# The second layer of a two-layer network woven between the first layer's mixtures, on one core

## The chip, the core and the metric

The kernel runs on one core of one Trainium2 chip. Its engines work side by side: PE (TensorE, matrix products into PSUM), DVE (VectorE), ACT (ScalarE), POOL (GpSimd) and SP, which issues most of the DMAs. Each engine takes its own instructions in order, and waits for the others through semaphores. The metric is the device time of one execution in microseconds.

## What is computed

4096 tokens of 128 numbers pass two layers. Each layer normalizes x, makes an attention-like signal s and a gate from a mixture of eight experts (the two best of eight for each token), and adds s * silu(gate) to x. In layer one s is linear attention; in layer two it is a recurrence that learns a matrix by one gradient step per token.

```python
xn = _layernorm(x)
s = _L0_attn_ref(xn, ...)          # relu(q)+eps, relu(k)+eps; q (k'v) z, times W_out, + b_out
g = _silu(_L0_ffn_ref(xn, ...))    # 8 experts of width 64, the 2 best
x = x + s * g
xn = _layernorm(x)
s = _L1_attn_ref(xn, ...)          # per token: pred = W k + b; g = 2/128 (pred - v)
                                   # W -= 0.01 g k'; b -= 0.01 g; out = W q + b   (from W0, b0)
g = _silu(_L1_ffn_ref(xn, ...))    # 8 experts of width 512, the 2 best
x = x + s * g
```

## The kernel before

The tokens lie in eight groups of 512 (`G`), each four tiles of 128; a group holds two sequences of 256.

**First layer.** `norm0` (L299) takes the statistics of a group on DVE (`stats`, L261), the root on ACT, normalizes on ACT into xn and turns it on PE into xnT (`turned`, L276). `attention` (L492) makes q (L494 on PE, evicted as qT by DVE at L496), then k and v tile by tile (kvp, L503; k by DVE, v by ACT), k'v (kw, L514) and s (sp, L520; s by DVE, L525). Its product also holds the logits of the first gate. After four groups `gate0` (L390) picks the two best experts on DVE and leaves `mask` and the factor `u`. `mixture0` (L531) turns the mask on PE (mp, L534), copies it twice on ACT (off, mT), computes all experts' hidden layers (hp: L543, with a small product, L547, that pushes unpicked experts down, then Gelu on ACT, L548), then the result (yp, L552 and L553). ACT scales it and takes its Tanh, and three DVE operations (L560 to L562) update x.

**Second layer, first part.** `second` (L792) works on a pair of groups: `norm1` (L317) takes the statistics on DVE, finds the root by Newton steps there (`inverse_root`, L284), normalizes on ACT into xw, turns it, and multiplies with WRO (rp, L343): the residual R and the output O of the recurrence's start, and the logits. A second product (L345, 24 rows, bfloat16) adds b0, split in three bfloat16 parts by `prepare` (L197). ACT copies rp to RO (L346). `dispatch` (L409) picks the two best experts on DVE, counts tokens per expert by products with triangles of ones (cp, L426 to L430), and computes each token's place. POOL then writes the rows of xw to these places with 16 indirect DMAs (L456). `keys` (L570) makes K (projk), Q (projq) and K'K (kk, L582), stored through `kk_hbm`. After each second pair `invert_blocks` (L592) inverts 32x32 blocks of four groups on DVE in 31 dependent steps.

**Second layer, second part.** `solve` (L619) runs the recurrence of a group in 14 steps of small products with DVE between them. `fetch`, `turn`, `hidden` and `result` take the slots of 256 dispatched tokens through one expert each, 39 in all; the steps of `solve` for groups 2 to 7 lie between them. Groups 0 and 1 are solved ahead of the slots. At the end the rows are gathered and x is updated (L851 to L853).

**Order.** The framework's planner orders each engine's instructions by its own estimate of when they are ready, starting from the order in which they are emitted. The emission (L776 to L807) is: attention of all eight groups with the gates after groups 3 and 7, then mixture 0, 1, 2, then for g = 2, 4, 6 the second layer's pair (g - 2, g - 1) after mixture g, and the last pair at the end. SP's queue holds, in order, the loads, the copies of the second layer's weights to `wts` (L154 to L160), 43 writes of zeros to `rows` (L166), then the traffic of `kk_hbm`, the blocks and the slots. Tiles come from pools with few buffers each: PSUM has three banks for h (kvp, hp, rp), two for y and three for t (turned tiles, mp, projk, projq, kk, cp), so a product also waits for an earlier eviction.

Of the kernel before, what the change touches and what calls it, by code (L numbers as in the profile page):

```python
# [21 lines left out]
P = 128  # L22
E = 8
# [32 lines left out]
def _constants():  # L56

    s = np.arange(P)[:, None]
    t = np.arange(P)[None, :]
    out = [t // BLK < s // BLK, s <= t]
    sel = np.zeros((P, 4 * P), bool)
    for e in range(E):  # L70
        sel[e, e * 64:(e + 1) * 64] = True
    out.append(sel)
    for row in (E - np.arange(E), np.arange(E * BATCH) % BATCH > 0, np.arange(NS), np.arange(E) * CAP * SLOT):
        out.append(np.broadcast_to(row[None, :], (P, row.size)))
    out.append(np.concatenate([s // E == np.arange(3), s % E == 0], axis=1))
    return np.concatenate(out, axis=1).astype(np.float32)
# [3 lines left out]
def tile_kernel(  # L80
# [57 lines left out]
    bias3 = p2.tile([3 * E, 2 * P], F32, tag="xgT", name="bias3")  # L138
    for k in range(3):
        nc.sync.dma_start(out=bias3[ts(k, E), 0:P], in_=b2_0)  # L140
# [4 lines left out]
    nc.sync.dma_start(out=bias3[:, P:], in_=b0.partition_broadcast(3 * E))  # L145
# [36 lines left out]
    third = consts_sb[0:3 * E, ds(at + 2 * E + E * BATCH + NS, 4)]  # L182
# [10 lines left out]
    starts = wp.tile([3 * E, P], BF16, tag="starts", name="starts")  # L193

    B0 = wp.tile([3 * E, 2 * P + E], BF16, tag="B0", name="B0")

    def prepare():  # L197

        n = 3 * E

        hi, mid = (p2.tile([n, 2 * P], BF16, tag=t, name=f"third_{t}") for t in ("e0", "e1"))
        a, acc = (p2.tile([n, 2 * P], F32, tag=t, name=f"third_{t}") for t in ("R2", "y"))
        V = nc.gpsimd
        V.tensor_copy(hi, bias3)
        V.tensor_tensor(a, bias3, hi, ALU.subtract)
        V.tensor_copy(mid, a)
        V.tensor_tensor(a, a, mid, ALU.subtract)
        V.tensor_scalar(acc, hi, third[:, 0:1], None, ALU.mult)
        V.tensor_scalar(bias3, mid, third[:, 1:2], None, ALU.mult)
        V.tensor_tensor(acc, acc, bias3, ALU.add)  # L210
        V.tensor_scalar(a, a, third[:, 2:3], None, ALU.mult)
        V.tensor_tensor(B2, acc[:, 0:P], a[:, 0:P], ALU.add)
        V.memset(B0, 0.0)
        for k in range(2):
            V.tensor_tensor(B0[:, ts(k, P)], acc[:, P:], a[:, P:], ALU.add)
        V.tensor_copy(starts, third[:, 3:4].to_broadcast([n, P]))
        V, late = nc.vector, tc.keep_in_program_order
        late(V.tensor_tensor(strict, upto, ident, ALU.subtract))

        late(V.tensor_scalar(sel_off, sel_sb, OFF, None, ALU.mult))  # L220

        for j in (1, 3):
            late(V.tensor_scalar(mKQ[:, j, :], upto, -ETA, None, ALU.mult))
        late(V.tensor_copy(free, region))
# [45 lines left out]
    def centre(mv, rstd, n):  # L270

        nb = p3.tile([P, n], F32, tag=f"nb{n}", name="nb")
        nc.vector.scalar_tensor_tensor(nb, mv[:, :, 0], -1.0, rstd, ALU.mult, ALU.mult)
        return nb
# [24 lines left out]
    def norm0(g):  # L299
        mv = p3.tile([P, 4, 2], F32, tag="mv", name=f"mv0_{g}")  # L300
        stats(g, mv, pinned=g > 0)
        if g == 0:

            rstd = inverse_root(mv[:, :, 1], 4)
        else:
            rstd = p3.tile([P, 4], F32, tag="rstd", name=f"rstd0_{g}")
            nc.scalar.activation(rstd, mv[:, :, 1], AF.Sqrt, bias=eps_t)
            nc.vector.reciprocal(rstd, rstd)
        nb = centre(mv, rstd, 4)
        xn = p2.tile([P, 4, P], F32, tag="xn", name=f"xn0_{g}")  # L310
        for i in range(4):
            nc.scalar.activation(
                xn[:, i, :], X[g][:, i, :], AF.Identity, bias=nb[:, i:i + 1], scale=rstd[:, i:i + 1]
            )
        return turned(0, g, xn)

    def norm1(q):  # L317

        mv = p3.tile([P, BATCH, 2], F32, tag="mv1", name=f"mv1_{q}")
        for h in range(2):  # L320
            stats(2 * q + h, mv[:, ts(h, 4), :])
        rstd = inverse_root(mv[:, :, 1], BATCH)
        nb = centre(mv, rstd, BATCH)
        out = []
        for h in range(2):
            g = 2 * q + h

            XW[g] = p3.tile([P, 2, 4, ROW], F32, tag="xw", name=f"xw{g}", bufs=4)
            xn = XW[g][:, 0, :, 0:P]
            for i in range(4):  # L330
                j = 4 * h + i
                nc.scalar.activation(  # L332
                    xn[:, i, :], X[g][:, i, :], AF.Identity, bias=nb[:, j:j + 1], scale=rstd[:, j:j + 1]
                )
            xnT = turned(1, g, xn)
            nc.gpsimd.tensor_copy(XW[g][:, 1, :, 0:P], xn)
            for k in range(2):
                nc.gpsimd.tensor_copy(XW[g][:, k, :, ROW - 1].bitcast(I32), to[:, ts(g, 4), k])
            if h == 0:
                RO = keep.tile([P, BATCH, 2 * P + E], F32, tag=f"RO{q}", name=f"RO{q}")  # L340
            for i in range(4):
                rp = ps_h.tile([P, 2 * P + E], F32, tag="h", name=f"rp{g}_{i}")
                nc.tensor.matmul(rp, lhsT=xnT[:, i, :], rhs=WRO, start=True, stop=False)  # L343

                nc.tensor.matmul(rp, lhsT=starts, rhs=B0, start=False, stop=True)  # L345
                nc.scalar.copy(RO[:, 4 * h + i, :], rp)  # L346
            out.append((xnT, RO[:, ts(h, 4), :]))
        return out, RO[:, :, 2 * P:].rearrange("p i e -> p e i")

# [59 lines left out]
    def dispatch(q, L):  # L409
# [14 lines left out]
        V.tensor_tensor(V1, SC, S, ALU.subtract)  # L424
        cp = ps_t.tile([P, E * n + E], F32, tag="t", name=f"cp{q}")
        nc.tensor.matmul(cp[:, 0:E * n], lhsT=strict, rhs=S.rearrange("p e i -> p (e i)"), start=True, stop=False)  # L426
        nc.tensor.matmul(cp[:, 0:E * n], lhsT=ones_sq, rhs=V1.rearrange("p e i -> p (e i)"), start=False, stop=True)
        last = tl("d_last", [P, E])
        V.tensor_copy(last, SC[:, :, n - 1])
# [62 lines left out]
    def attention(g, xnT, logits):  # L492
# [3 lines left out]
        nc.vector.tensor_scalar(qT, qp, 0.0, ATT_EPS, ALU.max, ALU.add)  # L496
# [31 lines left out]
        return s  # L528


    def mixture0(g, xnT, s, mask, u):  # L531
# [8 lines left out]
        hT2 = [p2.tile([P, 2, 4, P], F32, tag="hT", name=f"hT0_{g}_{h}") for h in range(2)]  # L540
        for q in range(4):
            hp = ps_h.tile([P, 4, P], F32, tag="h", name=f"hp0_{g}_{q}")
            nc.tensor.matmul(  # L543
                hp, lhsT=w1_0sb[:, ts(q, 2), :].rearrange("p e h -> p (e h)"), rhs=xnT, start=True, stop=False
            )

            nc.tensor.matmul(hp, lhsT=sel_off[:, ts(q, P)], rhs=off, start=False, stop=True)  # L547
            nc.scalar.activation(hT2[q // 2][:, q % 2], hp, AF.Gelu, bias=b1_0sb[:, q:q + 1])  # L548
        yp = ps_y.tile([P, 4, P], F32, tag="y", name=f"yp0_{g}")
# [5 lines left out]
        f = p2.tile([P, 4, P], F32, tag="U", name=f"f0_{g}")  # L555
        t = p2.tile([P, 4, P], F32, tag="T", name=f"t0_{g}")
# [13 lines left out]
    def keys(g, xnT):  # L570
# [5 lines left out]
        nc.scalar.copy(K, pp)  # L576
        qp = ps_t.tile([P, 4, P], F32, tag="t", name="projq" + n)
# [8 lines left out]
        return K  # L586
# [32 lines left out]
    def solve(g, Q, K, RO):  # L619
# [3 lines left out]
        D = DT[g % 3]  # L623
        for i in range(NB):
            q = ts(i, BLK)
            nc.sync.dma_start(out=D[q, :, q], in_=blk_by[g // 4, i, :, ts(g % 4, 4), :])
# [141 lines left out]
    def some(work, n):  # L768
        for _ in range(n):
            next(work, None)  # L770
# [4 lines left out]
    xnT0, s0, S0 = [], [], {}  # L775
    for g in range(G):  # L776
        if g % 4 == 0:
            logits0 = p2.tile([P, E, NT // 2], F32, tag="logits0", name=f"logits0_{g}")
        while len(xnT0) < min(g + 3, G):
            xnT0.append(norm0(len(xnT0)))  # L780
        s0.append(attention(g, xnT0[g], logits0))
        if g == 1:
            prepare()
        if g % 4 == 3:
            gate0(g // 4, logits0, mask, u)
    for j, th in enumerate((thK_sb, thQ_sb)):
        merged(j, th)


    XW, first, K1, blocks = {}, [], [], []  # L790

    def second(q):  # L792
        pair, logits = norm1(q)
        first.extend(pair)
        dispatch(q, logits)
        K1.extend(keys(g, first[g][0]) for g in (2 * q, 2 * q + 1))
        if q % 2:
            blocks.append(invert_blocks(q // 2))

    for g in range(G):  # L800
        mixture0(g, xnT0[g], s0[g], mask, u)
        if g >= 2 and g % 2 == 0:
            second(g // 2 - 1)
        if blocks:
            some(blocks[0], 10)
    some(blocks[0], BLK)
    second(G // 2 - 1)  # L807


# [85 lines left out]
```

## Time and profile before

| what | value |
|---|---|
| median of three runs | 533.08 us (531.45 to 534.18) |
| the profiled execution | 532.66 us, span 530.9 us |
| busy: PE, PEld, DVE, ACT, POOL | 444.9, 335.9, 261.7, 205.6, 161.5 us |
| attention, to about 77 us | PE busy 55.3 us |
| mixtures with the second layer's first part, 77 to 281 us | PE busy 177.2 us |
| slots, 307 to 500 us | PE busy 190.6 us |
| end, 500 to 531 us | PE busy 4.4 us |

PEld is the loading of weights into PE, which overlaps with products. A float32 product shows as two matmul records. In a timeline a row has start, length, engine, line and operation, output and inputs, count, and in brackets the idle time before it with the engine that ended it. In a group a row has the busy time, the mean in ns, and the idle time before. The clock of PE is given as a share of full speed, 1.00 or 0.50 at any moment, and in between as a mean.

### The profile page before, as it was taken

The numbers are of one execution on the slowest core, as the hardware profiler recorded it, in microseconds if no ns is written. First come the engines' busy times: TensorE is split into PE (matmuls) and PEld (weight loads), VectorE is DVE, ScalarE is ACT, GpSimd is POOL, SyncE is SP. The second block draws the span as 40 slices with busy tenths as digits, with TensorE's granted clock in tenths as the row PEclk, the third lists the DMA queues.
The fourth block names the chain that finished last, engine by engine and source line by source line (L and its number), as shares of the span: only waits on it lengthen the run. The fifth ranks groups of instructions, "written<-read, shape, count | busy, mean of one in ns | idle before, by whom it ended". The sixth has DMA issues, their size and how long they took to land.

```text
span 530.9 us, 7732 instructions
## 1 busy us (share of the span) xinstructions
PE 444.9 (84%) x2471; PEld 335.9 (63%) x2471; DVE 261.7 (49%) x1000; ACT 205.6 (39%) x476; POOL 161.5 (30%) x215
## 2 busy tenths in 40 slices
PE   2956999989989997993879499999999999999900
PEld 1635765634543563351358489999999989989900
DVE  4567573424160437574065149964445334334447
ACT  4455455442552535154221034333334423333321
POOL 3410000010750372037127214433424233434500
PEclk9997999967995997696569699999999999999965
DMA  9689997000310120022002575685766555545185
GB/s 237 154 166 299 393 392 280 1 0 2 125 35 1 60 71 11 0 72 77 7 30 81 178 191 155 194 238 149 225 191 187 144 171 155 186 145 178 36 313 166
DMA packets 59404, 75.64 MB, mean 142 GB/s; under 512 B 17100, under 2 KB 42364, under 8 KB 59364
## 3 DMA queue, kind: packets, MB, share of 16 engines
q1 hardware_dynamic: 51268, 62.30, 38.7%
q0 software_dynamic: 4544, 9.38, 5.1%
q10 hardware_dynamic: 3552, 3.48, 1.9%
q8 instruction: 19, 0.31, 0.2%
q14 instruction: 21, 0.17, 0.1%
HBM read 43.81 MB, written 36.06 MB: 150 GB/s over the span
## 4 chain that ended last, share of the span: by engine, by line
PE 57%; DMA 19%; SPq 8%; DVE 7%; ACT 4%; issue 3%; POOL 1%; ACTq 0%; DVEq 0%; POOLq 0%
PE yp L735 9%; PE hp L723 9%; DMA xg<-rows 9%; PE rp L343 7%; PE yp L552 7%; PE hp L543 6%; SPq L166 5%; DMA wts<-in_w_dram 4%; PE rp L345 2%; DMA fk<-res 2%; PE projq L578 2%; PE kk L582 2%; PE projk L574 2%; PE tp L279 1%; PE hp L547 1%
## 5 line engine op out<-in xcount | busy, mean ns | idle before, releaser
L744 POOL DMA_INDIRECT res<-y,go x78 | 75.7, 971 | 133.4 <-DVE y L742 109.3
L726 ACT ACTIVATE hT<-hp,wt 128x256 f32<-128x256 f32 x156 | 64.5, 470 | 113.7 <-issue 73.3
L456 POOL DMA_INDIRECT rows<-xw,place x64 | 63.0, 985 | 104.3 <-DVE xw L449 86.0
L735 PE MATMUL yp<-wt,hT 128*128 128x128 f32 x624 | 76.0, 275 | 0.0
L723 PE MATMUL hp<-xgT,wt 128*128 128x256 f32 x312 | 74.1, 381 | 1.9 <-DVE xgT L714 1.6
L735 PEld LDWEIGHTS yp<-wt,hT 128*128 128x128 f32 x624 | 72.8, 192 | 0.1
L723 PEld LDWEIGHTS hp<-xgT,wt 128*128 128x128 f32 x312 | 56.4, 190 | 8.9 <-DVE xgT L714 2.6
L343 PE MATMUL rp<-WRO,xnT 128*128 128x264 f32 x64 | 38.8, 709 | 4.0 <-ACT xnT L281 4.0
L543 PE MATMUL hp<-xnT,w_0sb 128*128 128x512 f32 x64 | 39.5, 728 | 1.4 <-ACT hT L548 1.4
L552 PE MATMUL yp<-w_0sb,hT 128*128 128x128 f32 x256 | 38.4, 290 | 0.0
L708 DVE COPY go<-xg 128x2 f32<-128x2 f32 x39 | 6.8, 175 | 63.6 <-DMA xg<-rows 63.5
L552 PEld LDWEIGHTS yp<-w_0sb,hT 128*128 128x128 f32 x256 | 31.7, 191 | 5.0 <-issue 2.8
L560 DVE SCALAR_TENSOR_TENSOR f<-t,f 128x512 f32<-128x512 f32 x8 | 5.5, 693 | 45.3 <-ACT t L559 45.3
L346 ACT COPY RO<-rp 128x264 f32<-128x264 f32 x32 | 12.1, 378 | 34.7 <-PE rp L345 34.7
L363 DVE TENSOR_REDUCE d_m_d<-RO 128x8 f32<-128x64 f32 x4 | 0.9, 220 | 46.8 <-ACT RO L346 46.8
L548 ACT ACTIVATE hT<-hp,b_0sb 128x512 f32<-128x512 f32 x32 | 21.1, 688 | 5.2 <-PE hp L547 4.9
L343 PEld LDWEIGHTS rp<-WRO,xnT 128*128 128x128 f32 x64 | 15.4, 299 | 11.9 <-ACT xnT L281 6.4
L740 DVE TENSOR_TENSOR y<-yp,wt 128x256 f32<-128x256 f32 x39 | 16.3, 419 | 12.1 <-PE yp L735 12.1
L279 PE MATMUL tp<-ident,xw 128*128 128x128 f32 x32 | 10.2, 394 | 14.4 <-ACT xw L332 14.1
L503 PE MATMUL kvp<-WKVG,xnT 128*128 128x264 f32 x64 | 19.6, 423 | 2.8 <-ACT v L505 2.3
L608 DVE TENSOR_TENSOR inv<-NBK,TB 64x31 f32<-64x31 f32 (+15 forms) x62 | 21.1, 341 | 0.8
L714 DVE COPY xgT<-xp 128x256 f32<-128x256 f32 x39 | 16.2, 416 | 10.6 <-PE xp L712 9.0
(239 smaller groups left out, 779.7 us busy)
## 6 DMA issues: line engine op xcount, KB each, us to landing
wt<-wts SPq DMA_DIRECT2D x39, 578.0 KB
rows<-pad SPq DMA_DIRECT2D x43, 390.0 KB
xg<-rows SPq DMA_DIRECT2D x39, 130.0 KB
wts<-in_w_dram SPq DMA_DIRECT2D x16, 256.0 KB
x<-in_x_dram SPq DMA_DIRECT2D x8, 256.0 KB
kk_hbm<-cb SPq DMA_DIRECT2D x8, 256.0 KB
B<-kk_hbm SPq DMA_DIRECT2D x8, 256.0 KB
fk<-res ACTq DMA_DIRECT2D x4, 512.0 KB
```

The lines of the kernel that those rows point to most:

```text
L166: nc.sync.dma_start(out=rows_q[q], in_=pad)
L343: nc.tensor.matmul(rp, lhsT=xnT[:, i, :], rhs=WRO, start=True, stop=False)
L456: nc.gpsimd.indirect_dma_start(out=parts_r[2 * (BATCH * q + i) + k], out_offset=IndirectOffsetOnAxis(ap=place[:, k, i:i + 1], axis=0), in_ ...
L503: nc.tensor.matmul(kvp, lhsT=xnT[:, i, :], rhs=WKVG, start=True, stop=True)
L543: nc.tensor.matmul(hp, lhsT=w1_0sb[:, ts(q, 2), :].rearrange("p e h -> p (e h)"), rhs=xnT, start=True, stop=False)
L548: nc.scalar.activation(hT2[q // 2][:, q % 2], hp, AF.Gelu, bias=b1_0sb[:, q:q + 1])
L552: nc.tensor.matmul(yp[:, i, :], lhsT=hT2[q // 2][:, q % 2, i, :], rhs=w2_0sb[:, q, :], start=(q == 0), stop=False)
L608: nc.vector.tensor_tensor(t, NBK[0:m, j, j + 1:].unsqueeze(1).to_broadcast(sh), TB[0:m, 0:j + 1, j].unsqueeze(2).to_broadcast(sh), ALU.mult,)
L723: nc.tensor.matmul(hp[:, c], lhsT=wt[:, ts(2 * c2 + c, P)], rhs=xgT, start=True, stop=True)
L726: nc.scalar.activation(hT[:, 2 * c2 + c], hp[:, c], AF.Gelu, bias=wt[:, j:j + 1])
L735: nc.tensor.matmul(yp[:, h, :], lhsT=hT[:, c, ts(h, P)], rhs=wt[:, ds(4 * P + c * P, P)], start=(c == 0), stop=(c == 3),)
L744: nc.gpsimd.indirect_dma_start(out=parts_y[2 * s + h], out_offset=IndirectOffsetOnAxis(ap=go[:, h, 1:2].bitcast(I32), axis=0), in_=y[:, h, ...
```

## The change

It cuts the first layer's mixture in two (`hidden0`, `result0`) and the second layer's first part for a pair of groups in five (`second`, now a generator), and emits these pieces in a new order. Hidden layers 0 to 3 and results 0 to 2 are emitted beside attention of groups 4 to 7. The rest is emitted piece by piece in a block in which the planner keeps PE's instructions in emitted order; the other engines' are still ordered by the planner. b0 is no longer added by a product: it is loaded to all partitions (`b0_bc`) and added to R and O at the start of `solve`. The statistics of the first layer are taken for groups 0, 1, 2 and 3, and 4 to 7 together (`spread0`). q's eviction moves from DVE to ACT (Relu) and POOL (add). `prepare` runs wholly on POOL. Some tiles share other buffers.

```diff
-    bias3 = p2.tile([3 * E, 2 * P], F32, tag="xgT", name="bias3")
+    bias3 = p2.tile([3 * E, P], F32, tag="xgT", name="bias3")
...
-    nc.sync.dma_start(out=bias3[:, P:], in_=b0.partition_broadcast(3 * E))
+    b0_bc = load(nc.sync, [P, P], b0.partition_broadcast(P), "b0_bc")
...
+    def spread0(gs):
+
+        n = 4 * len(gs)
+        mv = p2.tile([P, n, 2], F32, tag=f"mv{n}", name=f"mv0_{gs[0]}")
+        for h, g in enumerate(gs):
+            stats(g, mv[:, ts(h, 4), :], pinned=g > 0)
...
-            for i in range(4):
-                rp = ps_h.tile([P, 2 * P + E], F32, tag="h", name=f"rp{g}_{i}")
-                nc.tensor.matmul(rp, lhsT=xnT[:, i, :], rhs=WRO, start=True, stop=False)
-
-                nc.tensor.matmul(rp, lhsT=starts, rhs=B0, start=False, stop=True)
-                nc.scalar.copy(RO[:, 4 * h + i, :], rp)
+    def second(q):
+        pair = (2 * q, 2 * q + 1)
...
+            normed(g, XW[g][:, 0, :, 0:P], nb[:, ts(h, 4)], rstd[:, ts(h, 4)])
+        yield
...
+            xnT.append(turned(1, g, xn))
...
+                nc.tensor.matmul(rp, lhsT=xnT[h][:, i, :], rhs=WRO, start=True, stop=True)
                 nc.scalar.copy(RO[:, 4 * h + i, :], rp)
+            first[g] = xnT[h], RO[:, ts(h, 4), :]
+        yield
+        gate = dispatch(q, RO[:, :, 2 * P:].rearrange("p i e -> p e i"))
+        next(gate)
+        yield
+        for g in pair:
+            K1[g] = key(g, first[g][0])
+        for _ in gate:
+            pass
+        yield
+        for g in pair:
+            query(g, first[g][0], K1[g])
+        if q % 2:
+            blocks.append(invert_blocks(q // 2))
+        yield
...
-        nc.vector.tensor_scalar(qT, qp, 0.0, ATT_EPS, ALU.max, ALU.add)
+        nc.scalar.activation(qT, qp, AF.Relu)
+        nc.gpsimd.tensor_scalar(qT, qT, ATT_EPS, None, ALU.add)
...
+        for part in (R, O):
+            nc.vector.tensor_tensor(part, part, rep(b0_bc, 4), ALU.add)
...
+        if g >= 4:
+            hidden0(g - 4, xnT0[g - 4])
+        if g >= 5:
+            result0(g - 5, s0[g - 5])
+    S1 = [second(q) for q in range(G // 2)]
+
+    with tc.manual_schedule(engines={mybir.EngineType.PE}):
+        result0(3, s0[3])
+        next(S1[0])
+        hidden0(4, xnT0[4])
+        next(S1[0])
+        next(S1[0])
+        result0(4, s0[4])
+        next(S1[0])
+        next(S1[1])
+        hidden0(5, xnT0[5])
+        next(S1[0])
+        next(S1[1])
+        next(S1[1])
+        result0(5, s0[5])
+        next(S1[1])
+        next(S1[2])
+        hidden0(6, xnT0[6])
+        next(S1[1])
+        some(blocks[0], 6)
+        hidden0(7, xnT0[7])
+        next(S1[2])
+        next(S1[2])
+        result0(6, s0[6])
+        some(blocks[0], 6)
+        next(S1[2])
+        result0(7, s0[7])
+        next(S1[3])
+        some(blocks[0], BLK)
+        next(S1[2])
+        next(S1[3])
+        next(S1[3])
+        next(S1[3])
+        next(S1[3])
```

`dispatch` yields once, after DVE's part ahead of cp, so that PE's products of `key` come before cp. `merged`, which prepares WRO, is emitted after attention of group 3.

## The prediction

> **What bounds the kernel now.** I read first, on the page, where in the span PE works and at what granted clock:
>
> ```profile
> PE   2956999989989997993879499999999999999900
> PEclk9997999967995997696569699999999999999965
> ```
>
> One digit is 13.3 us. From slice 24 (305 us) PE is full at full clock until 500 us: the slots of the second layer's mixture, which the change leaves alone. Ahead of that the clock falls again and again. Busy times by stage tell where:
>
> ```profile
> 77.00:107.00 30.00, 29.60 (x148) 17.00 (x146) 13.36 (x54) 15.94 (x31) 1.12 (x4) 1.00 0.42 159
> 107.00:124.00 17.00, 14.52 (x35) 6.31 (x35) 3.40 (x12) 7.69 (x20) 1.97 (x4) 0.59 0.00 0
> 124.00:154.00 30.00, 28.53 (x134) 16.81 (x132) 13.34 (x58) 13.11 (x27) 16.82 (x20) 0.95 0.22 70
> 154.00:171.00 17.00, 14.39 (x33) 5.88 (x33) 3.59 (x11) 7.88 (x20) 1.33 (x2) 0.62 0.01 4
> 240.00:265.00 25.00, 15.20 (x32) 6.17 (x32) 5.82 (x27) 8.89 (x23) 11.12 (x15) 0.57 0.14 38
> 308.00:400.00 92.00, 92.00 (x664) 87.46 (x663) 56.78 (x200) 36.29 (x88) 33.60 (x34) 1.00 0.62 184
> ```
>
> Behind the length come the busy us of PE, PEld, DVE, ACT and POOL, then the clock. First-layer mixtures (77 to 107, 124 to 154) run dense at full clock; each start of a second-layer pair (107, 154, 201, 240) runs at about 0.6. The groups show what that costs:
>
> ```profile
> L343 PE MATMUL rp<-WRO,xnT 128*128 128x264 f32 x64 | 38.8, 709 | 4.0 <-ACT xnT L281 4.0
> L345 PE MATMUL rp<-B,starts 24*128 24x264 bf16 x32 | 12.7, 396 | 0.0
> L503 PE MATMUL kvp<-WKVG,xnT 128*128 128x264 f32 x64 | 19.6, 423 | 2.8 <-ACT v L505 2.3
> ```
>
> L343 and L503 have one shape, yet L343 takes 709 ns and L503 423, and every rp has an L345 behind it. Last, the timelines of PE, POOL and SP around the last pair:
>
> ```profile
> 248.39 2.40 PE L279 MATMUL tp<-ident,xw 128*128 128x128 f32 x6 [8.58 <-ACT xw L332]
> 268.50 0.66 PE L426 MATMUL cp<-d_s_d,strict 128*128 128x64 f32 x2 [4.24 <-DVE d_s_d L416]
> 275.21 1.13 POOL L456 DMA_INDIRECT rows<-xw,place  x1 [21.04 <-DVE xw L449]
> 296.83 0.42 SPq L699 DMA_DIRECT2D xg<-rows  x1
> 307.47 3.72 PE L723 MATMUL hp<-xgT,wt 128*128 128x256 f32 x16
> ```
>
> From the last first-layer result (239.6) it is one chain: X, statistics, xw, rp, dispatch, 16 indirect writes 1.26 us apart (275.2 to 295.3), the first fetch, the first slot. It takes 67.9 us. So what comes before 307.5 counts in full, the rest keeps its length.
>
> **Part by part.** The order is read from the changed kernel's built instruction streams.
>
> *b0 out of rp.* An rp now costs 1.51 us (111.04 to 112.55). Without L345 it is L503's shape: 0.445 us apart at full clock (43.57 on). Bounds: 0.445 and the 1.18 us of an L343 pair at half clock. I take 0.445 where hidden layers surround it (first three pairs, 24) and 0.8 for the last eight, which follow a long idle. The load of b0 grows from 24 to 128 rows of 512 bytes at 15 us, far ahead of its use. In exchange DVE gets 16 adds of 128x512 (0.692 each, as L561; 11 us), most placed early, while PE is busy.
>
> *First mixtures beside attention.* Costs per group at full clock, from PE's timeline: qp 0.86, four kvp 1.8, kw 0.9, sp 0.9, tp 0.44, mask turn 0.44, hidden 4 x 1.37 = 5.5, result 4 x 1.245 = 5.0. Up to 42 us the order is no better than now: PE's first tp of group 4 stands ahead of group 2's kw and waits for the statistics of four groups (16 pairs at 0.40 = 6.4 us of DVE), the first gate's DVE work woven in (6 us) and two table loads (2 x 1.28). That puts it near 42 us; now qp of group 4 starts at 41.76. Behind that tp stand kw of groups 2 and 3 and qp of group 4, so two s and everything after wait with it. Such waits exist today:
>
> ```profile
> 38.95 0.86 PE L279 MATMUL tp<-ident,xn 128*128 128x128 f32 x2 [2.89 <-ACT xn L312]
> 49.97 0.86 PE L279 MATMUL tp<-ident,xn 128*128 128x128 f32 x2 [3.60 <-ACT xn L312]
> ```
>
> Then ACT sets the pace: 16 xn of 0.40, four xnT of 0.48, kws, qT, v, mask copies, the Gelu table and four Gelus come to 16.5 us and bring hidden layer 0 to 59.5. From there PE has 0.44 + 3 x 10.4 (qp, kvp, kw, sp, mask, hidden) + 4 x 5.0 = 51.6 us, ACT only some 7 per group: result 3 ends at **112**, with 1 us for evictions. Today results 0 to 2 end at 107.0, so this part gains 5 us (one mixture of 10.9 less 5).
>
> *qT* leaves DVE (8 x 0.687). ACT gets 8 Relu (0.58 to 0.64, as L281 and L559), POOL 8 adds on 128x512: between 0.61 (L336's copy) and 1.8 us (twice the 0.91 of a 24x256 tensor_scalar); I take 1.8, the same operation. sp reads qT 8 us after qp (13.64, 21.92), which hides both; uncovered it would be 2.4 us per group.
>
> *prepare* moves 1.2 us from DVE to POOL, idle there. Sel_off and B2 are needed after 50 us.
>
> *Second layer in five parts.* PE from result 3 to result 7: four hidden with masks 23.7, four results 20.0, three pairs' tp 2.6, 24 rp 10.7, six projk 5.2, four projq 3.4, four kk 3.6, three cp 1.5: 70.7 us. Waits in the emitted order: 1.3 before hidden 4's bias (ACT does f and tanh of group 3 first), 0.5 at each of three rp starts (xnT copy behind a Gelu), 2 since RO copies and xw share ACT, and 3.6 at the mask turn of group 7, which needs a PSUM buffer whose copy stands behind eight xw that wait for DVE. Queued behind that are hidden 7 and rp of pair 2. Together 8.4: result 7 ends at 112 + 79.1 = **191**. Gates are covered: 4.3 us of DVE (264.7 to 269.0) plus adds, against result and projk (6.7). Dispatches come 22 us apart or more against 20.2 of POOL; their indirect writes start near 137, after the pads (issued until 84) have landed. SP's other queue entries (kk_hbm, B, DT) keep their order.
>
> *The last chain*, 67.9 now: +0.6 for a copy ahead of tanh; +4.5 since the block inversion is woven into X, statistics and root on DVE (f to nb 6.1 now, 10.6 then); -6.2 on xw to the last RO (17.0 now; 3.8 + 6.5 + 0.5 then); +2.7 on the gate (15 inversion steps in it); -1.2 on cp; +0.7 for an add in the place computation; +0.4 after the fetch: **69.4**.
>
> Sum: 112 + 79.1 + 69.4 = 260.5 for the first slot, plus 3.5 for two returns of the clock after waits (today 38 to 42 us ran at 0.53 to 0.61: some 3.5 us at half, 1.75 lost), 264, against 307.5: 43.5 us less. The profiled execution took 532.66 (span 530.9), so **489**; it lies 0.4 below the median shown.
>
> The clock: PE sat idle at 107.7 and 109.6 for 1.1 and 0.7 us, and from 110 to 127 the clock was 0.50, PE being 16.3 of 17 us busy; six hidden-layer matmuls (123.4 to 128) ended it. [...] By the rows small waits can halve a whole stage: that is rival 4.
>
> **Rivals.**
> 1. *The emitted order waits more than I see* (0.22). For: PE can no longer fill a wait with later work, and ACT is queued in order with 69 us of work in 79. Against: hidden and result stand between nearly all producers and consumers. 1.5 us more at each of 12 hand-overs: 507.
> 2. *rp stays at half clock* (0.10): 24 x (0.9 - 0.445) = 11, and 2 to 3 us of each following result: 509. For: it is so now. Against: no L345, and 5.5 dense us before.
> 3. *Fewer waits than counted* (0.08): none of the 8.4 in the emitted order, none of the 3.5 for the clock, group 4 reached 7 earlier: 470.
> 4. *Slower: the clock stays half through the emitted-order stage* (0.05). Place: result 3 to result 7. Price: pairs of hidden matmuls took 1.55 at half (six in 4.66) and 0.86 at full clock, a factor 1.8, so 70.7 us become 127: 546. It decides once the added time passes 43.5 us, with 54 of the 70.7 us of work at half clock. Now 80 of 174 us (107 to 281) are at half clock, but never a mixture beyond its first 4 us.
> 5. *It doesn't do what it says*: attention remains bound by its chains, and mixtures add to it. Then result 3 ends near 118: 495, inside my range and part of the forecast's chance.
>
> **Numbers.** Forecast 489, chance 0.55 (478 to 500); rivals 0.22, 0.10, 0.08, 0.05. Range 474 to 511: it takes in rivals 1 and 2 and part of 3. A difference of 0.5% is about what a measurement of this kernel can tell from none; all cases but rival 4 lie far below it: faster 0.93, same 0.02, slower 0.05.
>
> **What would show it.** Right: rp pairs of matmuls about 0.45 us apart at clock 1.00; result 3 ending near 112, result 7 near 191, the last indirect writes starting near 231, the first slot near 264, then the same 193 us of slots. Wrong: a clock of 0.5 between 120 and 190; PE waits over 2 us there other than the mask of group 7; PE reaching group 4 later than 45; DVE's inversion holding up nb of the last pair by more than 5 us.

## The result, and the profile after

| | before | changed |
|---|---|---|
| median of 4 runs, us | 533.63 (531.45 to 534.4) | 483.62 (483.18 to 485.4) |
| profiled execution, us (span) | 532.66 (530.9) | 484.07 (482.3) |
| granted clock, mean of the span | 0.883 | 0.936 |

The ratio is 0.9075, 95% interval 0.9038 to 0.9112: 9.2% faster. Ratios leave out one slow execution, in e9 (520.22 us, the other three took 506.77 to 509.0). First the two rows of the page again, one digit for 12.1 us:

```profile
PE   0975999999999899188839999999999999899800
PEclk9995999999999999777979999999999999999965
```

Slices are counted from 0 here. Between attention and the last chain the clock row of the kernel before fell to 5 to 7 in slices 8, 9, 12, 15 and 16; now it shows 9 from 48 to 193 us; what is left is one hole (PE idle from 32.7 to 42 us, in slices 2 and 3) and a broken stretch in slices 16 to 20 (193 to 253 us), the last chain. The busy times of the changed kernel's stages (length, then PE, PEld, DVE, ACT, POOL, the clock, the DMA share and GB/s): up to group 4's first transpose, up to result 3, up to result 7, up to the first slot:

```profile
20.00:42.05 22.05, 12.68 (x68) 9.24 (x66) 16.53 (x84) 11.46 (x30) 9.29 (x18) 0.83 0.83 167
42.05:113.70 71.65, 71.64 (x368) 48.72 (x369) 30.70 (x129) 40.56 (x96) 9.59 (x19) 0.96 0.67 249
113.70:190.20 76.50, 72.38 (x351) 45.35 (x350) 44.50 (x188) 47.93 (x109) 36.33 (x45) 1.00 0.18 53
190.20:257.40 67.20, 43.51 (x216) 33.31 (x216) 44.04 (x167) 17.72 (x40) 33.60 (x36) 0.80 0.32 98
```

The third line is the emitted-order stage: PE idle for 4.1 of 76.5 us, the clock 1.00 throughout. The groups of rp (L343) and its twin in attention (L516) are now close, 442 and 405 ns where they were 709 and 423:

```profile
L343 PE MATMUL rp<-WRO,xnT 128*128 128x264 f32 x64 | 18.0, 442 | 0.9 <-ACT xnT L273 0.9
L516 PE MATMUL kvp<-WKVG,xnT 128*128 128x264 f32 x64 | 17.9, 405 | 0.1
```

And the timelines of PE, POOL and SP around the last pair, with the idle time ahead in brackets:

```profile
203.65 3.17 PE L271 MATMUL tp<-ident,xw 128*128 128x128 f32 x8 [9.79 <-ACT xw L309]
218.53 0.41 PE L440 MATMUL cp<-d_s_d,strict 128*128 128x64 f32 x2 [3.56 <-DVE inv L633]
225.09 0.98 POOL L468 DMA_INDIRECT rows<-xw,place  x1 [10.86 <-issue]
246.51 0.42 SPq L726 DMA_DIRECT2D xg<-rows  x1
249.34 2.07 PE L680 MATMUL e11p<-e,MT 128*128 128x128 f32 x8 [7.54 <-DVE e L698]
257.40 3.72 PE L750 MATMUL hp<-xgT,wt 128*128 128x256 f32 x16
```

Result 7 ends at 190.2, and the same chain follows: the wait for xw (9.8 us), rp, the gate, the last writes from 225.09, the first fetch, the first slot at 257.40. From there to the end it takes 224.9 us, 1.5 more than before.

### The profile page after: what moved, and what is told of

Read it like the earlier page. It is cut to its first block, busy times and chain, and to the rows that moved or that the text cites. A ratio compares the mean times of both kernels' runs of the same rounds, so it can differ in the third digit from the quotient of the medians.

```text
span 482.3 us, 7682 instructions
## 1 busy us (share of the span) xinstructions
PE 403.3 (84%) x2439; PEld 326.5 (68%) x2439; DVE 260.1 (54%) x995; ACT 206.8 (43%) x479; POOL 175.2 (36%) x224
## 3 DMA queue, kind: packets, MB, share of 16 engines
q10 hardware_dynamic: 3552, 3.48, 2.1%
## 4 chain that ended last, share of the span: by engine, by line
PE 57%; DMA 14%; DVE 12%; issue 5%; POOL 4%; SPq 3%; ACT 3%; ACTq 0%; DVEq 0%; POOLq 0%
PE hp L750 12%; PE yp L762 11%; PE yp L573 6%; PE hp L560 5%; DMA xg<-rows 5%; POOL rows L468 4%; PE rp L343 2%; DMA rows<-xw,place 2%; PE hp L564 2%; PE kvp L516 2%; DMA wts<-in_w_dram 2%; PE kw L527 1%; DMA fk<-res 1%; PE xp L739 1%; PE tp L271 1%
## 5 line engine op out<-in xcount | busy, mean ns | idle before, releaser
L750 PEld LDWEIGHTS hp<-xgT,wt 128*128 128x128 f32 x312 | 56.3, 190 | 10.2 <-DVE xgT L741 3.9
L573 PE MATMUL yp<-w_0sb,hT 128*128 128x128 f32 x256 | 36.7, 286 | 0.0
L560 PE MATMUL hp<-xnT,w_0sb 128*128 128x512 f32 x64 | 35.2, 632 | 0.0
L509 POOL TENSOR_SCALAR qT<-qT 128x512 f32<-128x512 f32 x8 | 11.9, 1492 | 38.2 <-ACT qT L508 38.0
L517 DVE TENSOR_SCALAR k<-kvp 128x128 f32<-128x128 f32 x32 | 9.1, 287 | 29.9 <-PE kvp L516 29.8
L650 DVE TENSOR_TENSOR RO<-RO,b_bc 128x512 f32<-128x512 f32 x16 | 10.8, 686 | 25.3 <-ACT RO L344 25.3
L741 DVE COPY xgT<-xp 128x256 f32<-128x256 f32 x39 | 16.1, 415 | 11.3 <-PE xp L739 9.6
L637 DVE TENSOR_TENSOR TB<-TB,inv 64x31 f32<-64x31 f32 (+15 forms) x62 | 20.3, 328 | 0.7
L579 ACT ACTIVATE f<-yp,u 128x128 f32<-128x128 f32 x32 | 9.2, 369 | 26.1 <-PE yp L574 26.1
L769 DVE TENSOR_SCALAR y<-y,go 128x128 f32<-128x128 f32 x78 | 18.9, 280 | 0.5
L256 DVE BATCH_NORM_STATS2 st<-x 128x6 f32<-128x128 f32 x64 | 16.6, 266 | 4.4 <-DMA x<-in_x_dram 4.3
```

The costliest lines, as they stand in the source:

```text
L256: b = nc.vector.bn_stats(st, X[g][:, i, :])
L560: nc.tensor.matmul(hp, lhsT=w1_0sb[:, ts(q, 2), :].rearrange("p e h -> p (e h)"), rhs=xnT, start=True, stop=False)
L573: nc.tensor.matmul(yp[:, i, :], lhsT=hT2[q // 2][:, q % 2, i, :], rhs=w2_0sb[:, q, :], start=(q == 0), stop=False)
L637: nc.vector.tensor_tensor(TB[0:m, 0:j + 1, j + 1:], TB[0:m, 0:j + 1, j + 1:], t, ALU.add)
L750: nc.tensor.matmul(hp[:, c], lhsT=wt[:, ts(2 * c2 + c, P)], rhs=xgT, start=True, stop=True)
L769: nc.vector.tensor_scalar(y[:, h, :], y[:, h, :], go[:, h, 0:1], None, ALU.mult)
```

## The experiments

Each kernel was run beside the kernel before on its chip; a ratio is to those runs, with its 95% interval. Three marks of each profiled execution say where the time lies: the end of result 2, from there to the end of result 7, and from there to the first slot.

| kernel | ratio | result 2 | to result 7 | to first slot |
|---|---|---|---|---|
| before | 1 | 107.2 | 132.6 | 67.7 |
| e1 b0 moved, nothing else | 0.9686 (0.9645 to 0.9726) | 106.5 | 118.5 | 63.8 |
| e9 before, b0's product on 128 rows | 0.9589 (0.9506 to 0.9673) | 106.6 | 114.6 | 61.1 |
| e11 changed, order of before | 0.9353 (0.9279 to 0.9428) | 101.4 | 110.8 | 59.4 |
| e6 changed, parts together | 0.9262 (0.9221 to 0.9302) | 107.0 | 95.8 | 60.3 |
| changed | 0.9075 (0.9038 to 0.9112) | 108.7 | 81.5 | 67.2 |
| e2 changed, b0's product back | 0.9315 (0.9276 to 0.9354) | 107.9 | 90.6 | 68.5 |
| e3 changed, planner orders PE | 0.9065 (0.9019 to 0.9110) | 107.9 | 76.6 | 71.6 |
| e4 changed, mixtures after attention | 0.9077 (0.9017 to 0.9138) | 106.3 | 80.2 | 68.5 |
| e5 changed, qT on DVE | 0.9116 (0.9066 to 0.9167) | 106.3 | 81.7 | 67.6 |
| e7 changed, inversion left out | 0.8968 (0.8904 to 0.9032) | 108.1 | 81.5 | 61.1 |
| e8 changed, statistics earlier | 0.8976 (0.8914 to 0.9038) | 101.8 | 80.8 | 67.8 |
| e12 e8 and later keys | 0.8830 (0.8784 to 0.8875) | 101.3 | 79.2 | 62.4 |
| e13 e12, PE kept busy | 0.8802 (0.8775 to 0.8828) | 102.1 | 81.1 | 62.4 |

**e1: b0 alone.** In the kernel before, with b0 loaded to all partitions:

```diff
+    b0_bc = load(nc.sync, [P, P], b0.partition_broadcast(P), "b0_bc")
...
-                nc.tensor.matmul(rp, lhsT=xnT[:, i, :], rhs=WRO, start=True, stop=False)
-                nc.tensor.matmul(rp, lhsT=starts, rhs=B0, start=False, stop=True)
+                nc.tensor.matmul(rp, lhsT=xnT[:, i, :], rhs=WRO, start=True, stop=True)
...
+        for part in (R, O):
+            nc.vector.tensor_tensor(part, part, rep(b0_bc, 4), ALU.add)
```

> The kernel before with one part of the change alone: no 24-row product behind rp, b0 added in the recurrence; order, stages and first layer stay as before. Theory (the half clock behind each start of a pair comes from the waits ahead of it, not from the 24-row product): only the product's own time goes, 32 x 0.396 us = 12.7, so 519 to 526 us; rp (64 records) stays above 0.62 us in the mean and the granted clock at the four pair starts stays at 0.5 to 0.65. Rival (the 24-row product itself holds the clock down): rp falls to 0.45 us, the clock there is above 0.9, and the time falls by 12.7 and by 64 x (0.709 - 0.445) = 17 more, to about 503 us.

513.76 us, 17 less than 530.68: between the two. rp fell to 518 ns, and the first pair's stage ran at full clock, although PE now waits more in it (7.33 of 10 us busy); the second start still fell to 0.50, but for 3.5 us only:

```profile
109.00:119.00 10.00, 7.33 (x26) 4.54 (x26) 7.89 (x27) 5.22 (x15) 1.14 (x3) 1.00 0.00 1
145.50:149.30 3.80, 1.61 (x5) 0.70 (x5) 1.77 (x3) 3.76 (x11) 1.20 (x5) 1.00 0.05 18
149.30:152.80 3.50, 3.21 (x8) 2.52 (x8) 1.82 (x9) 2.33 (x7) 0.67 (x2) 0.51 0.00 0
```

So the waits alone do not explain 17 us at 0.50, which was the theory; the 24-row product has a share.

**e2: the product back in the changed kernel.** The buffers `starts` and `B0` come back, and:

```diff
-                nc.tensor.matmul(rp, lhsT=xnT[h][:, i, :], rhs=WRO, start=True, stop=True)
+                nc.tensor.matmul(rp, lhsT=xnT[h][:, i, :], rhs=WRO, start=True, stop=False)
+                nc.tensor.matmul(rp, lhsT=starts, rhs=B0, start=False, stop=True)
...
-        for part in (R, O):
-            nc.vector.tensor_tensor(part, part, rep(b0_bc, 4), ALU.add)
```

> The changed kernel with the 24-row product put back behind every rp and without the adds in the recurrence. Theory: at clock 1.00 one such product costs about half of the 0.396 us that it took before, 24 x 0.2 for the first three pairs and 8 x 0.4 for the last, 8 us of PE at most, while DVE is relieved of 16 adds of 0.686: 486 to 492 us, the clock 1.00 from 120 to 190. Rival (the product holds the clock down): the clock falls to about 0.5 at the rp stages, rp is above 0.65 us, and the time is above 500 us.

494.77 us, 13 more than 0.9075 of that chip's 530.68 (481.6) and above the 486 to 492 expected, while the clock stayed where theory had it. The rp stage of pair 0, and the last pair behind its 10.5 us wait; then the starts of two rp of pair 0:

```profile
121.00:128.00 7.00, 6.80 (x24) 3.10 (x24) 0.00 (x0) 5.97 (x16) 0.61 (x1) 1.00 0.00 0
213.00:231.00 18.00, 18.00 (x36) 7.25 (x35) 10.10 (x32) 7.19 (x19) 8.09 (x11) 0.50 0.13 39
121.20 0.71 PE L349 MATMUL rp<-WRO,xnT 128*128 128x264 f32 x2 [0.24 <-ACT xnT L279]
122.06 0.71 PE L349 MATMUL rp<-WRO,xnT 128*128 128x264 f32 x2
```

Seven us of it at full clock do not pull the clock down: the rival falls. But an rp with its product came every 0.855 us (121.20, 122.06, 122.91), without it in the changed kernel every 0.445 (122.52, 122.97, 123.41): the product costs 0.41, not the 0.2 expected. 24 of them make 9.8 us of PE; result 2 to result 7 grew by 9.1. And where the clock was down, it stayed at 0.50 for 18 us of a fully busy PE; in the changed kernel it came back after 8.5 us (203.65 to 212.1).

**e9: 128 rows in place of 24**, in the kernel before, the added rows filled with zeros:

```diff
-    starts = wp.tile([3 * E, P], BF16, tag="starts", name="starts")
-    B0 = wp.tile([3 * E, 2 * P + E], BF16, tag="B0", name="B0")
+    starts = wp.tile([P, P], BF16, tag="starts", name="starts")
+    B0 = wp.tile([P, 2 * P + E], BF16, tag="B0", name="B0")
...
```

> The kernel before with the product of b0 behind every rp padded with zeros from 24 to 128 rows: as many instructions, the same columns and type, all rows of the array in use. The product of 24 rows left the clock at 0.50 for 17 us behind the first pair's start, and without it the clock was 1.00 there. Theory (few rows in use is what keeps the clock down): the clock returns within some 5 to 9 us of each start, rp falls from 709 to 550 ns or less, and the time falls to 505 to 520 us. Rival (the number of short products or their change of type keeps it down): rp stays near 700 ns, the clock at 0.50 for 15 us and more, 528 to 534 us.

506.77 to 509.0 us against 531.14: zeros in 104 more rows made the kernel before 4% faster, no less than taking the product out did (e1). Just as many products stand at the same places, and rp went from 709 to 467 ns, the product from 396 to 309. Behind the two groups stand the first pair's stage, the second start, and two rp at full clock:

```profile
L344 PE MATMUL rp<-WRO,xnT 128*128 128x264 f32 x64 | 23.4, 467 | 4.0 <-ACT xnT L282 4.0
L346 PE MATMUL rp<-B,starts 128*128 128x264 bf16 x32 | 9.9, 309 | 0.0
109.00:119.00 10.00, 8.01 (x34) 4.73 (x34) 5.89 (x24) 5.40 (x15) 1.23 (x3) 1.00 0.00 1
149.70:152.60 2.90, 2.90 (x9) 1.74 (x8) 1.14 (x8) 1.49 (x4) 0.61 (x1) 0.50 0.03 6
109.91 0.61 PE L344 MATMUL rp<-WRO,xnT 128*128 128x264 f32 x2
110.47 0.61 PE L344 MATMUL rp<-WRO,xnT 128*128 128x264 f32 x2
```

The second start lost the clock again, and had it back after 3.4 us, where the kernel before had 0.50 for 17.1 us at each of its first three starts. Number and type of the products are cleared: the few rows are what counts. They also set the price at a given clock: an rp with its product of 128 rows came every 0.56 us at full clock, 0.11 more than without, and every 1.10 at 0.50 (150.45, 151.55), where 24 rows took 0.855 and 1.51. Whether the clock answers to the few rows themselves or to the time that PE loses around such a product was not tested.

**e11: the order of before in the changed kernel**, all mixtures behind attention, PE left to the planner:

```diff
+        for g in range(G):
+            hidden0(g, xnT0[g])
+            result0(g, s0[g])
+            if g >= 2 and g % 2 == 0:
+                some(S1[g // 2 - 1], 5)
...
```

> The changed kernel in the order of emission of the kernel before: all of attention, then mixture after mixture, a whole pair of the second layer behind mixtures 2, 4 and 6, PE's order left to the planner. What stays changed is b0, the statistics taken together, qT, the buffers, and the order of work within a pair (both groups' xw, then both transposes, then 16 rp, gate, keys, queries). With the parts together but a mixture later it took 0.926 of the kernel before; with b0 alone 0.969. Theory (work within a pair is what shortened the waits, the place of the pair matters little): 0.92 to 0.935, some 488 to 496 us. Rival (the place is what matters, since a pair that follows mixture 2 waits for X of group 1 and ACT): 0.945 to 0.965, 502 to 512 us.

**e6: each pair's five parts together**, behind results 3, 4, 6 and 7, PE left to the planner:

```diff
         result0(3, s0[3])
+        some(S1[0], 5)
         hidden0(4, xnT0[4])
         result0(4, s0[4])
+        some(S1[1], 5)
...
```

> The changed kernel with the five parts of each pair emitted one behind the other, a whole pair after results 3, 4, 6 and 7 as in the kernel before, and PE's order left to the planner; b0, the first mixtures beside attention and qT stay changed. Theory (first-layer matmuls between the parts keep PE from waiting, and so the clock at 1.00): PE waits again for xw, for the gate and for X of the next group, the clock falls to about 0.5 to 0.7 at the pair starts, rp is above 0.55 us, and the time is 500 to 512 us. Rival (the planner fills these waits by itself, and the gain came from b0 and from the first mixtures): rp 0.44 to 0.48 us and 484 to 492 us.

e11 took 497.17 us, a ratio of 0.9353: just outside its theory's 0.92 to 0.935, and clear of the rival's 0.945. Against e1 it gains 5.1 us up to result 2, 7.7 up to result 7 and 4.4 in the last chain: the statistics of four groups together, then the work within a pair (xw of both groups, all transposes, eight rp in a row) with its buffers; these two were not taken apart. e6 took 490.54 us, as its rival had it: rp at 459 ns, and the clock at 0.50 in the stage only from 174.6 to 181.4 us. So the planner fills much of the waits by itself. Between e6 and the changed kernel lie 14.3 us of the stage, of which the last chain gives back 6.9 (60.3 to 67.2), where pair 2's keys and queries and the block inversion now run late (e7 and e12 take them out). The profiled execution of e6 was its fastest, 3.7 us below its median, so the marks show less of a difference than the ratios do. By the ratios the way from the kernel before goes down 3.1 points with b0 (e1), 3.3 with the statistics and the work within a pair (e11), 0.9 with the place of a pair (e6) and 1.9 with mixing the parts with mixtures, some 17, 18, 5 and 10 us.

**e3: PE's order left to the planner.**

```diff
-    with tc.manual_schedule(engines={mybir.EngineType.PE}):
+    if True:
```

> The changed kernel emitted in the same order, with PE's order left to the planner. In its instruction stream the last results 4 to 6 are split around rp, three hidden matmuls run ahead of their 8-row partners, and result 7 is split around cp. Theory (the order of emission matters, who keeps it does not): 482 to 488 us. Rival (keeping the emitted order is what saves the time, since the planner's estimates send PE into waits): above 491 us, with waits of 2 us and more between 120 and 190 and a clock below 1.00 there.

480.89 us, 0.9065: no difference. PE waited 0.7 us in the stage instead of 4.1, and the last chain grew by 4.4. Having PE keep the emitted order neither costs nor gains; the order of emission is what gains (e6).

**e4: first mixtures behind attention.**

```diff
-        if g >= 4:
-            hidden0(g - 4, xnT0[g - 4])
-        if g >= 5:
-            result0(g - 5, s0[g - 5])
...
+    for g in range(3):
+        hidden0(g, xnT0[g])
+        if g:
+            result0(g - 1, s0[g - 1])
+    hidden0(3, xnT0[3])
+    result0(2, s0[2])
```

> The changed kernel with hidden layers 0 to 3 and results 0 to 2 emitted behind all of attention instead of beside it; everything behind that is as changed. Theory of the prediction (this part is worth 5 us, since attention then runs at its own pace and the mixtures follow dense): the ratio to the kernel before goes from 0.9075 to about 0.917, some 487 us on this chip, and PE waits in attention as in the kernel before. Rival (attention alone leaves PE waiting for ACT and DVE for longer than that, so this part is worth more): 10 us and more, 492 us or above, with PE idle over 8 us more between 42 and 115 us.

480.54 us, 0.9077: the overlap is worth nothing, and both theories fall. Attention from group 4 on, and then the four mixtures, without any overlap; last, about the same part of attention in the kernel before:

```profile
41.56:68.00 26.44, 26.43 (x154) 22.48 (x155) 12.94 (x60) 16.36 (x47) 7.30 (x12) 0.90 1.01 371
68.00:111.30 43.30, 43.30 (x215) 25.13 (x214) 18.65 (x72) 25.63 (x51) 3.80 (x10) 1.00 0.49 185
42.00:73.09 31.09, 25.91 (x135) 19.87 (x134) 19.62 (x97) 14.09 (x40) 1.83 (x9) 0.89 1.01 370
```

PE is full in both, so there was nothing to fill. In the kernel before, that part took 31.1 us with PE 25.9 busy. The 5 us are those waits, 3.6 of them for an xn (at 49.97). They are gone in e11 too (result 2 at 101.4, in e1 106.5), so what removed them is in what e11 shares with the changed kernel: the statistics taken together, qT, `prepare` and the buffers. e5 rules out qT. The statistics are the likely one, since the waits were for xn; no run undoes them alone.

**e5: qT on DVE again.**

```diff
-        nc.scalar.activation(qT, qp, AF.Relu)
-        nc.gpsimd.tensor_scalar(qT, qT, ATT_EPS, None, ALU.add)
+        nc.vector.tensor_scalar(qT, qp, 0.0, ATT_EPS, ALU.max, ALU.add)
```

> The changed kernel with qT evicted by one DVE instruction again, in place of Relu on ACT and an add on POOL. The prediction counted this move at nothing: 0.6 us of ACT and 1.5 us of POOL per group lie ahead of a product that comes 8 us later, and so would 0.69 us of DVE. Theory: no difference, 0.902 to 0.913 of the kernel before, result 3 ending within 1.5 us of 113. Rival (the 5 us by which attention became shorter, which the mixtures beside it do not explain, came from DVE being free of qT): result 3 ends near 118, 486 us and more.

0.9116, its interval overlapping the changed kernel's; result 3 ended at 111.3, 1.7 us earlier than expected and not later. No difference in time, as predicted.

**e7: the first inversion left out.**

```diff
-        for j in range(BLK - 1):
+        for j in range((0, BLK - 1)[half]):
```

> The changed kernel with the 31 elimination steps of the first block inversion (groups 0 to 3) left out, so that part of the recurrence is not computed and only the time tells. Theory of the prediction (these steps, woven into DVE's work, cost the last chain 4.5 us between f and nb and 2.7 us in the gate): f to nb of the last pair falls from 10.6 to about 6 us, the last indirect writes start 6 to 8 us earlier, and so does the first slot: 473 to 477 us on this chip. Rival (the solves, the fetches and POOL's writes behind it take the gain back): the writes start earlier, the first slot less than 3 us.

475.00 us. From f of the last group to nb, the shift of the last pair's normalization, it took 6.1 us instead of 10.6; the last writes started 29.0 us behind result 7 instead of 34.9, and the first slot came 6.1 sooner behind it. Nothing took the gain back. But the gate did not get shorter: from d_m to d_last it took 6.1 us, in the changed kernel 5.2, since two adds of b0 now stood in it. What came beside the 4.5 us was won ahead of it, from nb to d_m (9.5 us instead of 11.3). The wait for xw:

```profile
198.54 3.17 PE L271 MATMUL tp<-ident,xw 128*128 128x128 f32 x8 [5.25 <-ACT xw L309]
```

**e8: the statistics earlier**, for two groups at a time, and the root on DVE; the two were not taken apart.

```diff
+        if g in (0, 1):
+            gs = [2 * g + 4, 2 * g + 5]
+            spread.update(zip(gs, spread0(gs)))
```

> The changed kernel with the statistics of groups 4 and 5 emitted behind attention 0, those of 6 and 7 behind attention 1, and the Newton root on DVE for these groups in place of the Sqrt table. In the profile of the changed kernel PE waits 9.4 us for the first xn of group 4. Theory (that wait is only the late statistics and two table loads, and all before 115 us hangs on it): group 4's first tp starts near 34 us, and the time falls by 5 to 8 us, to about 474 us on this chip (ratio to the kernel before 0.892 to 0.898). Rival (ACT's work sets the pace from there to hidden layer 0, so that the wait moves on): less than 2 us.

475.40 us, as expected. Group 4's first transpose came at 33.94, and in the 22 us in which the changed kernel had PE busy for 12.7 it was now busy for 21.2, at full clock:

```profile
20.00:42.05 22.05, 21.23 (x122) 15.98 (x120) 18.44 (x114) 15.70 (x44) 8.44 (x17) 1.00 0.79 166
```

**e12: the version from these.** e8; the queries of pair 1 ahead of hidden layer 6, pair 2's rp and gate ahead of hidden layer 7, its keys and queries behind result 7:

```diff
         next(S1[2])
+        next(S1[1])
         hidden0(6, xnT0[6])
...
+        next(S1[2])
+        next(S1[2])
         hidden0(7, xnT0[7])
         next(S1[2])
         result0(6, s0[6])
         result0(7, s0[7])
         next(S1[3])
+        next(S1[2])
...
```

> A version meant to beat both: the earlier statistics of e8, the queries of pair 1 ahead of hidden layer 6 (so that the block inversion starts earlier), pair 2's rp and gate ahead of hidden layer 7, and its keys and queries behind result 7, where PE waited 9.8 us for the last pair's xw. Theory (that wait is filled with 7 us of PE work which then no longer stands ahead of result 7): the last pair's first tp near 190 us instead of 196, the first slot near 244 instead of 250, 466 to 471 us, a ratio of 0.880 to 0.888 to the kernel before. Rival (DVE, with 20 of the 31 inversion steps still between f and nb, sets the last chain, and the work only moves): 472 to 476 us, as e8.

468.87 us, 0.883, as expected: faster than both kernels, 2.7% below the changed one by the ratios (0.883 / 0.9075). The first slot came at 242.90. DVE is now what sets the start of the last chain: it was busy for 13.0 of the 13.05 us between result 7 and the next transpose.

**e13: PE kept busy in that wait.**

```diff
+        idle = ps_y.tile([P, 4, P], F32, tag="y", name="idle")
+        for _ in range(8):
+            nc.tensor.matmul(idle, lhsT=thQ_sb, rhs=first[4][0], start=True, stop=True)
```

> The version of e12 with eight 128x512 matmuls whose result nobody reads, 6.9 us at full clock, put between the queries of pair 2 and the last pair's first transpose, where PE sat idle for 7.6 us; behind that idle time tp, rp and projk ran at clock 0.50 (3.17, 5.48 and 1.88 us). Theory (the idle time alone sets the clock back, and only dense work of full rows keeps it): the clock stays at 1.00 up to the wait for the gate, rp takes 3.8 to 4.0 us and tp below 2.0, so the gate, the last writes and the first slot come 2 to 3 us earlier: 465 to 467 us where e12 took 468.9. Rival (the chain is set by ACT's copies and DVE behind the first rp, or the clock falls anyway): 468 to 470 us.

469.41 us, 0.8802: no gain that can be told from e12's interval. The eight matmuls held the clock, but the transposes behind them come at the pace of ACT's xw, and after 3.8 us with ACT 3.69 and PE 2.63 busy it fell all the same. From that first transpose to projk it took 8.5 us (196.16 to 204.65), as in e12 (193.55 to 202.03). There the clock was 0.50 from 190 to 200 us, and 1.00 again for projk (1.88 us in both). The stretches of e13:

```profile
188.50:195.50 7.00, 7.00 (x18) 2.82 (x16) 7.00 (x37) 0.69 (x1) 5.38 (x6) 1.00 0.36 124
195.50:199.30 3.80, 2.63 (x9) 1.11 (x8) 3.49 (x11) 3.69 (x10) 2.92 (x3) 1.00 0.17 55
199.30:202.80 3.50, 3.48 (x8) 2.76 (x9) 3.26 (x8) 1.64 (x4) 2.57 (x5) 0.51 0.12 38
```

## Why the prediction was right, and where it was not

| step | predicted | measured |
|---|---|---|
| group 4's first transpose | 42 | 42.05 |
| hidden layer 0 done | 59.5 | 61.2 |
| result 3 ends | 112 | 113.7 |
| result 3 to result 7 | 79.1 | 76.5 |
| result 7 to first slot | 69.4 | 67.2 |
| two returns of the clock | 3.5 more | none left over |
| first slot | 264 | 257.4 |
| end | 489 | 484.07 |

The profile came out 5.1 us below the sum (532.66 - 43.5): +1.7 up to result 3, -2.6, -2.2, -3.5, and +1.5 in the slots. That it came so close is in part luck: errors of both signs, and one gain that came by another way than forecast.

- *b0 out of rp*: the sizes held, 0.445 us from one rp to the next in the first three pairs, as predicted, and 0.78 in the last (0.8; 6.27 us for eight, 206.81 to 213.08). The step put the whole way from 1.51 us down to one cause. It has two: 0.41 us is the product itself at full clock (e2), the rest the clock that it held down (e9). Taken alone, the edit brought 17 us and left the waits bare (e1).
- *First mixtures beside attention*: "this part gains 5 us (one mixture of 10.9 less 5)" is the step that failed. The 5 us came (4.4: result 3 ended 6.5 us behind the old result 2, with a mixture of 10.9 more in it), but not by the overlap, as e4 shows; they went with the waits for xn, most likely through the statistics taken together. The bracket does not give 5 either: 10.9 less 5 is 5.9. The prediction counted PE work and ACT work for an overlap, but did not ask whether attention by itself, once group 4 was reached, would leave PE any idle time.
- *qT and prepare*: nothing, as counted (e5). The add on POOL took 1.49 us, within its bounds of 0.61 and 1.8.
- *The second layer in five parts*: right, with waits of 4.1 us instead of 8.4. The wait for group 7's mask was 1.8 us, not 3.6; those at the rp starts were 0.24 to 0.44. Rival 1 (the emitted order waits more) did not come, nor did its opposite matter: the planner's order takes as long (e3).
- *The last chain*: f to nb 10.6 as predicted and shown by e7; xw to the last RO 10.6 (10.8 predicted). The mis-sized term is the gate, +2.7 predicted and +1.5 measured: d_m to d_last took 5.2 us, 4.4 before, and began 0.7 late behind one inversion step. In DVE's timeline most of the woven steps lie between two gate steps of which one needs the other. That the inversion costs the gate anything is argued from this: in e7 the gate was no shorter, with two adds in place of the steps. The other 1.0 us of the 2.2 is made of differences below 0.4.
- *The clock*: 3.5 us were set aside for two returns. One lies in the 1.7 us up to result 3 (0.50 from 34.6 to 48.3 us), the other was in the 0.8 us for the last eight rp already: it was counted twice.
- *Rivals 2 and 4* rested on "small waits can halve a whole stage". The runs correct this. Behind 3.0 to 3.8 us with PE busy only for 42 to 69% the clock was 0.50 (e1, e11, e13), but among rp it was back after 3.4 us when the product had 128 rows (e9), and after 17.1 with 24.

## What to carry to other kernels

Before work is put beside a stage, read PE's busy time in that stage as it will then stand: where it is full, the overlap only moves work, and here it gained nothing (0.9077 without it in e4, 0.9075 with it). An order of emission that keeps a chain's steps a matmul stage apart was worth some 10 us here (e6), and whether the scheduler or the author kept it mattered little (e3). A small side product on few rows is worth trying on 128 rows, or on another engine: here padding took its price from 0.41 to 0.11 us at full clock, and the 0.50 at the second pair's start from 17.1 to 3.4 us (e9).

## What was not expected of the hardware

- The clock fell without a long wait: in e11 after 3.0 us with PE 2.08 us busy, in e13 after 3.8 with 2.63, in e1 after 3.8 with 1.61. No single wait in these was above 1.61 us. It did not fall in e1 when PE was busy for 0.7 us between 107.0 and 109.5 (1.00 from 109 to 119), nor behind a wait of 2.6 us at 117.3 (two projk matmuls behind it took 1.08 us), nor in e6 behind one of 3.1 at 145.6 (two projq matmuls, 1.08). The stretch of e11:

```profile
103.00:106.00 3.00, 2.08 (x7) 1.10 (x8) 2.35 (x5) 3.00 (x7) 2.26 (x4) 1.00 0.00 0
106.00:109.30 3.30, 3.30 (x9) 2.46 (x8) 0.94 (x8) 1.36 (x5) 0.16 (x1) 0.50 0.00 0
```

- It stayed at 0.50 for different times. Up to the first slot these were, in the changed kernel, 13.7 us from 34.6 and from 198.5 on, 6.8 from 219.0 and from 246.3; in the kernel before 3.4 us from 38.5 on, 6.8 from 48.7, 17.1 from 110.1, 157.9 and 205.7, 30.7 from 243.3 and 10.2 from 294.5. What decides when it falls was not settled.
- It came back after 3.3 to 3.5 us of matmuls of 128 rows in e11 (106.0 to 109.3, PE busy throughout), e1 (3.21 of 3.50 us busy) and e13 (3.48 of 3.50). In the changed kernel it took 8.5 us behind the 9.8 us wait, with PE busy throughout, on transposes and rp of 128 rows too. With 24-row products in the mix it was 0.50 for all 18 us from 213 to 231 (e2), with 128-row ones for 3.4 (e9).
- A product of 24 rows and 264 columns between two rp cost 0.41 us at full clock (e2), more than its own record of 0.28. Padded to 128 rows, with a record as long, it cost 0.11 (e9).
